# A state-space layer on one core: products with B three steps ahead of their decay instead of two

## The chip, the cores and the metric

The kernel runs on one core of a Trainium2 chip. The metric is the device time of one execution in microseconds (us). Everything is in fp32.

## The reference

The input is `x`, eight images of 128 channels by 128 by 128 pixels. Two layers follow each other. The first (a dilated convolution, a two-dimensional Fourier transform, attention between channels and a gate in the frequency domain) is left as it is by the change. The second layer is what matters:

```python
y = conv2d(x, conv_w, 3x3, padding 1) + conv_b
seq = y.reshape(B * H * W, 8, 16)            # every pixel-row stretch of 128 values: 8 tokens of 16
xi, z = split(seq @ in_proj_w.T)             # 32 and 32 channels
xc = silu(causal_conv1d(xi, 4 taps))
dt, Bm, Cm = split(xc @ x_proj_w.T, [1, 16, 16])
dt = softplus(dt * dt_proj_w + dt_proj_b)
h = 0
for t in range(8):                           # 32 channels x 16 states
    h = exp(dt[t] * A) * h + dt[t] * Bm[t] * xc[t]
    ys[t] = sum(h * Cm[t], over the states)
out = ((ys + D * xc) * silu(z)) @ out_proj_w.T
return x + silu(group_norm(out))
```

The recurrence over eight tokens is done for every pixel position. Per token there are three elementwise products or sums over 32 channels x 16 states: the decay `exp(dt*A) * h`, the sum with the injected `dt*x*B`, and the weighting with C.

## The kernel before, in words

The second layer (`layer1`) walks over 256 blocks of four image rows. A block is `N = 512` columns, and its 512 rows of state (32 channels x 16 states) are held as four groups of 128 partitions. Two groups make one tile of 128 x 1024, so the eight tokens are cut into sixteen steps `s` of two groups each: token `s // 2`, and the first or second pair of groups by `k = s % 2` (`GP = 2`).

For each step these are the operations, and the names that the text uses:

- `spreads(das, upss)` (its product is line 800). TensorE spreads `dt` over channels and states with the matrix `m_a`, into the PSUM tile `da`; and `u = dt * x` with the matrix `m_u`, into the PSUM tile `ups`. The moving operand of both is `du`, where each of the four groups has 32 partitions of its own, with eight rows of `dt` and eight of `u` in the first sixteen. A product uses the sixteen rows from `a = (k * GP + q) * 32`, for `q` 0 and 1. So a spread of one decay and one injection is four products of 16 rows with 512 columns.
- `exps` (line 805): ScalarE takes the exponential of `da` in place.
- `inject` (line 815): VectorE multiplies `ups` with B (`bb`, laid out by DMA) into a new SBUF tile `h`.
- `decay` (lines 829 and 831): VectorE multiplies `da` with the `h` of the step two before.
- `add` (line 839 on VectorE, or 837 on GpSimd for the steps 4, 7 and 10): adds the decayed state to the injected `h`.
- `weigh` (line 845): GpSimd multiplies `h` with C (`cc`) into `hc`; `last_decay` (line 850) is its counterpart for the last token, on VectorE; `collect` (line 866) sums `hc` over the states on TensorE.

The steps 14 and 15 have no injection of their own, since the last token's injected part is summed another way (`end_products`, `ends_sum`, `ends_inputs`). There are fourteen decays (2 to 15) and fourteen injections (0 to 13) in a block.

The order on every engine is written out by hand. `step(i, s)` for s from 2 to 11 issues the spread with the decay of step s+1 and an injection further ahead, the other TensorE work that is laid into this step (projections of the next block, gathers, convolution taps of the block three ahead), then VectorE's decay, sum and injection for the step. `seam(i)` writes out the end of block i (decays 12 to 15) together with the first injections of block i+1.

Buffers set the waits. `ups` has one PSUM buffer, so a spread's injection products wait until the injection before them was read by VectorE. `da` has two buffers, shared with the x and z projections (lines 736 and 745). `h` has six SBUF buffers; `pm`, for convolution, projections and transposes, has one PSUM buffer. The DMA transfers that lay out `du`, `bb` and `cc` are issued from one queue in the order of the code: `lay_du` and `lay_states` for the next block in steps 6 and 10 and at the seam.

Of the kernel before, what the change touches and what calls it, by code (L numbers as in the profile page):

```python
# [589 lines left out]
def layer1(ctx, tc, x1, w1, c1, out):  # L590
# [22 lines left out]
    def cf(name):  # L613
        at, n = C1[name]
        return ct[:, at:at + n]
# [21 lines left out]
    taps = cf("taps").rearrange("p (k l) -> p k l", l=L)  # L637
# [41 lines left out]
    wk1 = ctx.enter_context(tc.tile_pool(name="l1_w1", bufs=1))  # L679
    wk2 = ctx.enter_context(tc.tile_pool(name="l1_w2", bufs=2))  # L680
    wk3 = ctx.enter_context(tc.tile_pool(name="l1_w3", bufs=3))
    hp = ctx.enter_context(tc.tile_pool(name="l1_h", bufs=6))
    hcp = ctx.enter_context(tc.tile_pool(name="l1_hc", bufs=7))
    p_u = ctx.enter_context(tc.tile_pool(name="l1_pu", bufs=1, space=PSUM))
    p_a = ctx.enter_context(tc.tile_pool(name="l1_pa", bufs=2, space=PSUM))
# [10 lines left out]
    def live(i):  # L696
        return 0 <= i < nb
# [4 lines left out]
    def load(i):  # L702
        b, r = blocks[i]
        if r % CH == 0:
            lo, hi = max(0, r - 1), min(H, r + CH + 1)
            xin = wk2.tile([P, CH + 2, W], F32, name="xin")
            nc.sync.dma_start(xin[:, :hi - lo, :], x1[b][:, lo:hi, :])
            xins[b, r // CH] = xin, lo
        st8[i]["xin"] = xins[b, r // CH]
# [20 lines left out]
    def pair():  # L730
        return p_a.tile([P, GP, N], F32, name="da")
# [55 lines left out]
    def spreads(das, upss):  # L787

        todo = []
        for m, name, k0, steps in ((m_a, "da", 0, das), (m_u, "ups", 0, upss)):  # L790
            for i, s in steps:
                if not live(i):
                    continue
                d, t, k = st8[i], s // GP, s % GP
                d[name, s] = pair() if name == "da" else p_u.tile([P, GP, N], F32, name="ups")
                for q in range(GP):
                    a = (k * GP + q) * 32
                    todo.append((d[name, s][:, q], m[a:a + 16, :], d["du", t // LP][a:a + 16, t % LP, :]))
        for o, w, v in todo:
            nc.tensor.matmul(o, w, v, start=True, stop=True)  # L800

    def exps(i, s):
        if live(i):
            da = st8[i]["da", s]
            nc.scalar.activation(da, da, AF.Exp)  # L805

    def state_row(i, name, t):
        return st8[i][name, t // LP][:, t % LP:t % LP + 1, :].broadcast_to([P, GP, N])

    def inject(i, s):  # L810
        if not live(i):
            return
        d = st8[i]
        h = hp.tile([P, GP, N], F32, name="h")
        nc.vector.tensor_mul(h, d["ups", s], state_row(i, "bb", s // GP))  # L815
        d["h", s] = h
# [24 lines left out]
    def weigh(i, s, t):  # L841

        d = st8[i]
        hc = hcp.tile([P, GP, N], F32, name="hc")
        nc.gpsimd.tensor_mul(hc, d["h", s], state_row(i, "cc", t))  # L845
        d["hc", t * GP + s % GP] = hc

    def last_decay(i, s):
        d = st8[i]
        nc.vector.tensor_mul(d["hc", s], d["da", s], d["hc", s])  # L850
# [7 lines left out]
    def ends_inputs(i, hf):  # L858
        d = st8[i]
        nc.vector.tensor_mul(d["yps"], d["yps"], d["u", hf])  # L860
# [40 lines left out]
    def norm_of(b):  # L901

        mv = wk2.tile([P, 2], F32, name="mv")
        gmv = wk2.tile([P, 2], F32, name="gmv")
        dv = wk2.tile([P, 1], F32, name="dv")
        sc = wk2.tile([P, 1], F32, name="sc")
        bi = wk2.tile([P, 1], F32, name="bi")
        nc.vector.bn_aggr(mv, stats[b])
        ps = misc().rearrange("p a b -> p (a b)")
        nc.tensor.matmul(ps[:, 0:2], cf("group"), mv, start=True, stop=True)  # L910
        nc.vector.tensor_copy(gmv, ps[:, 0:2])
        nc.vector.tensor_sub(dv, mv[:, 0:1], gmv[:, 0:1])
        nc.vector.tensor_mul(dv, dv, dv)
        ps = misc().rearrange("p a b -> p (a b)")
        nc.tensor.matmul(ps[:, 0:1], cf("group"), dv, start=True, stop=True)
        nc.vector.tensor_scalar(sc, ps[:, 0:1], gmv[:, 1:2], GN_EPS, ALU.add, ALU.add)
        nc.scalar.activation(sc, sc, AF.Sqrt)
        nc.vector.reciprocal(sc, sc)
        nc.vector.tensor_mul(sc, sc, wf("gn_w"))
        nc.vector.tensor_mul(bi, gmv[:, 0:1], sc)  # L920
        nc.vector.tensor_sub(bi, wf("gn_b"), bi)
        tails.extend((b, r, sc, bi) for r in range(0, H, RB))
# [22 lines left out]
    def step(i, s):  # L945

        now, nxt = live(i), live(i + 1)
        if s == 2:
            if live(i + 4):
                load(i + 4)  # L950
            if live(i - 2) and blocks[i - 2][1] + RB == H:
                norm_of(blocks[i - 2][0])
        spreads([(i, s + 1)], [(i, s + 2)])
        exps(i, s + 1)

        if s == 2:
            if nxt:
                project_dt(i + 1, 0)
            if live(i - 1):
                collect(i - 1, 7)  # L960
        elif s == 3:
            if live(i - 1):
                collect(i - 1, 6)
                skip(i - 1, 1)
            if nxt:
                project_bc(i + 1, 0)
        elif s == 4 and nxt:
            project_dt(i + 1, 1)
        elif s == 5:
            if now:  # L970
                ends_sum(i, 0)
            if nxt:
                project_bc(i + 1, 1)
        elif s == 6:
            if now:
                skip(i, 0)
            if live(i - 1):
                project_out(i - 1, 0, 4)
        elif s == 7 and now:
            collect(i, 1)  # L980
        elif s == 8 and live(i - 1):
            project_out(i - 1, 4, 8)
        elif s == 9 and now:
            collect(i, 2)
        elif s == 11 and now:
            collect(i, 3)
        if s in CONV and live(i + 3):
            conv(i + 3, *CONV[s])

        if now:  # L990
            decay(i, s)
            if s != 4:
                add(i, s)
            inject(i, s + 2)
            if s == 5:
                ends_inputs(i, 0)
            if s == 11:
                gated(i, 0)
        if s == 3 and live(i - 1):
            gated(i - 1, 1)  # L1000

        if now:
            if s == 2:
                end_products(i, 0)
            else:
                weigh(i, s - 1, (s - 1) // GP)
            if s == 4:
                add(i, s)
            if s == 7:
                end_products(i, 1)  # L1010
        if s in (3, 4) and nxt:
            inputs(i + 1, s - 3)
        if s == 9 and "active" in fin:
            last_sum()

        if s == 3 and now:
            lay_states(i, 1, 1)
        elif s == 6 and nxt:
            lay_du(i + 1, 0)
            lay_states(i + 1, 0, 0)  # L1020
        elif s == 8 and tails:
            last_load()
        elif s == 10 and nxt:
            lay_states(i + 1, 0, 1)

    def seam(i):


        now, nxt = live(i), live(i + 1)

        def taps(k0, k1):
            if live(i + 3):
                conv(i + 3, k0, k1)

        spreads([(i, 13)], [(i + 1, 0)])
        exps(i, 13)
        if now:
            ends_sum(i, 1)
            decay(i, 12)
            add(i, 12)  # L1040
            weigh(i, 11, 5)
            weigh(i, 12, 7)
        if nxt:
            lay_states(i + 1, 1, 0)
        taps(5, 6)
        if "loaded" in fin:
            last_act()
        if live(i + 2):
            project_x(i + 2)
        if now:  # L1050
            decay(i, 13)
            add(i, 13)
            weigh(i, 13, 7)
        inject(i + 1, 0)
        if live(i + 2):
            project_z(i + 2)
        spreads([(i, 14)], [(i + 1, 1)])
        exps(i, 14)
        if now:
            ends_inputs(i, 1)  # L1060
        inject(i + 1, 1)
        taps(6, 8)
        spreads([(i, 15)], [(i + 1, 2)])
        exps(i, 15)
        if live(i - 1):
            keep(i - 1)
        inject(i + 1, 2)
        if now:
            collect(i, 4)
            last_decay(i, 14)  # L1070
        taps(8, 9)
        if now:
            weigh(i, 12, 6)
            last_decay(i, 15)
        spreads([(i + 1, 2)], [(i + 1, 3)])
        exps(i + 1, 2)
        inject(i + 1, 3)
        if now:
            collect(i, 5)
            weigh(i, 13, 6)  # L1080
        if live(i + 3):
            turn(i + 3)
        if nxt:
            lay_du(i + 1, 1)
# [95 lines left out]
```

## Time and profile before

| what | value |
|---|---|
| time | 14902.07 us, median of 3 runs (14893.55 to 14902.99) |
| TensorE products busy | 96% of the span |
| GpSimd busy | 87% |
| VectorE busy | 85% |
| ScalarE busy | 56% |
| first and last product with `m_u` | 2068.9 us and 14740.4 us |

Shares are of the whole span, and the first layer, some 2000 us, has other limits than the second. The shares inside the second layer are read from windows of its own. A product in the trace is an instruction with a start and a modelled end; one fp32 product of the program appears as two such instructions, one after the other.

### The profile page before, as it was taken

The numbers are of one execution on the slowest core, as the hardware profiler recorded it, in microseconds if no ns is written. First come the engines' busy times: TensorE is split into PE (matmuls) and PEld (weight loads), VectorE is DVE, ScalarE is ACT, GpSimd is POOL, SyncE is SP. The second block draws the span as 40 slices with busy tenths as digits, with TensorE's granted clock in tenths as the row PEclk, the third lists the DMA queues.
The fourth block names the chain that finished last, engine by engine and source line by source line (L and its number), as shares of the span: only waits on it lengthen the run. The fifth ranks groups of instructions, "written<-read, shape, count | busy, mean of one in ns | idle before, by whom it ended". The sixth has DMA issues, their size and how long they took to land.

```text
span 14895.3 us, 200912 instructions
## 1 busy us (share of the span) xinstructions
PE 14287.1 (96%) x70696; PEld 5588.1 (38%) x70696; DVE 12683.2 (85%) x12417; ACT 8294.9 (56%) x9234; POOL 12983.2 (87%) x7076
## 2 busy tenths in 40 slices
PE   9999999999999999999999999999999999999996
PEld 6677653333333333333333333333333333333331
DVE  3343359999999999999999999999999999999995
ACT  3354355555555555565655555555555555555553
POOL 6666668989999999999999999999999999999996
PEclk9999999999999999999999999999999999999997
DMA  4444456666666666666666666666666666666665
GB/s 136 139 139 122 129 124 117 120 118 121 130 137 134 137 132 136 133 135 134 135 136 133 136 133 137 133 138 131 137 133 136 132 137 133 134 135 135 136 133 140
DMA packets 1091885, 1976.01 MB, mean 133 GB/s; under 512 B 125760, under 2 KB 256832, under 8 KB 1082688
## 3 DMA queue, kind: packets, MB, share of 16 engines
q1 hardware_dynamic: 1090304, 1960.82, 61.0%
q8 instruction: 563, 9.22, 0.3%
q14 instruction: 442, 3.62, 0.1%
q10 hardware_dynamic: 576, 2.35, 0.0%
HBM read 419.16 MB, written 201.33 MB: 42 GB/s over the span
## 4 chain that ended last, share of the span: by engine, by line
PE 72%; DVE 18%; issue 4%; ACT 4%; DMA 1%; POOL 0%; SPq 0%; DVEq 0%; POOLq 0%; ACTq 0%
PE da L800 19%; PE yps L866 9%; PE ups L800 7%; PE pm L134 7%; DVE da L831 6%; PE m L280 4%; DVE h L839 4%; DVE h L815 4%; PE yps L872 4%; PE pm L752 4%; PE pm L885 3%; PE pm L764 3%; DVE hc L850 2%; PE da L745 2%; PE yps L856 2%
## 5 line engine op out<-in xcount | busy, mean ns | idle before, releaser
L845 POOL TENSOR_TENSOR hc<-h,cc 128x1024 f32<-128x1024 f32 x3584 | 8377.2, 2370 | 427.6 <-DVE h L839 408.5
L805 ACT ACTIVATE da<-da 128x1024 f32<-128x1024 f32 x3584 | 3618.7, 1010 | 4193.3 <-PE ups L800 2491.7
L815 DVE TENSOR_TENSOR h<-ups,bb 128x1024 f32<-128x1024 f32 x3584 | 4368.7, 1219 | 690.1 <-PE ups L800 313.9
L800 PE MATMUL da<-du,m_a 16*128 16x512 f32 x14336 | 4068.1, 644 | 140.5 <-DVE hc L850 135.1
L800 PE MATMUL ups<-du,m_u 16*128 16x512 f32 x14336 | 4114.3, 642 | 2.5 <-DVE h L815 1.4
L839 DVE TENSOR_TENSOR h<-da,h 128x1024 f32<-128x1024 f32 x2304 | 2821.2, 1224 | 79.1
L831 DVE TENSOR_TENSOR da<-da,h 128x1024 f32<-128x1024 f32 x2304 | 2820.1, 1224 | 6.8 <-ACT da L805 3.3
L134 PE MATMUL pm<-xin,l_wt 128*128 128x508 f32 (+1 forms) x4608 | 2412.7, 624 | 177.0 <-ACT xr L890 170.2
L837 POOL TENSOR_TENSOR h<-ah,h 128x1024 f32<-128x1024 f32 x768 | 1818.8, 2368 | 451.2 <-DVE ah L829 409.6
L800 PEld LDWEIGHTS da<-du,m_a 16*128 16x128 f32 x14336 | 1078.4, 184 | 2624.6 <-issue 1002.7
L866 PE MATMUL yps<-hc,l_ct 128*32 128x512 f32 x14336 | 1931.7, 611 | 0.0
L134 PEld LDWEIGHTS pm<-xin,l_wt 128*128 128x128 f32 x4608 | 751.7, 189 | 1620.7 <-issue 1396.0
L800 PEld LDWEIGHTS ups<-du,m_u 16*128 16x128 f32 x14336 | 1124.4, 184 | 380.8 <-DVE h L815 298.2
L805 ACT ACT_TABLE_LOAD x774 | 993.0, 1283 | 30.1 <-PE ups L800 1.3
L829 DVE TENSOR_TENSOR ah<-da,h 128x1024 f32<-128x1024 f32 x768 | 933.1, 1215 | 0.0
L759 POOL TENSOR_TENSOR u<-dt,xc 128x512 f32<-128x512 f32 x512 | 656.0, 1281 | 190.2 <-ACT dt L754 190.2
L866 PEld LDWEIGHTS yps<-hc,l_ct 128*32 128x32 f32 x14336 | 283.6, 108 | 1375.1 <-issue 968.6
L754 ACT ACT_TABLE_LOAD x511 | 655.6, 1283 | 29.6 <-PE pm L752 2.1
L822 POOL TENSOR_TENSOR cb<-bb,cc 128x512 f32<-128x512 f32 x512 | 658.3, 1286 | 11.8 <-DMA cc<-bc 11.8
L885 PEld LDWEIGHTS pm<-m_o,ym 128*128 128x128 f32 x4096 | 517.6, 191 | 317.2 <-issue 316.5
L850 DVE TENSOR_TENSOR hc<-da,hc 128x1024 f32<-128x1024 f32 x512 | 600.6, 1215 | 0.9 <-ACT da L805 0.8
L872 PE MATMUL yps<-xc,m_d 128*128 128x512 f32 x1024 | 584.6, 653 | 0.0
(180 smaller groups left out, 14537.5 us busy)
## 6 DMA issues: line engine op xcount, KB each, us to landing
bb<-bc SPq DMA_DIRECT2D x2048, 256.0 KB
cc<-bc SPq DMA_DIRECT2D x2048, 256.0 KB
du<-dt SPq DMA_DIRECT2D x2048, 64.0 KB
du<-u SPq DMA_DIRECT2D x2048, 64.0 KB
xin<-x SPq DMA_DIRECT2D x152, 768.0 KB
xin<-x SPq DMA_DIRECT2D x112, 640.0 KB
gn<-xr SPq DMA_DIRECT2D x256, 256.0 KB
v<-gn SPq DMA_DIRECT2D x256, 256.0 KB
```

The lines of the kernel that those rows point to most:

```text
L134: nc.tensor.matmul(out[:, a:b, wa:wb], wt[:, t, :], src[:, r + dy + a - base:r + dy + b - base, wa + dx:wb + dx], start=(n == 0), stop=(n ...
L800: nc.tensor.matmul(o, w, v, start=True, stop=True)
L805: nc.scalar.activation(da, da, AF.Exp)
L815: nc.vector.tensor_mul(h, d["ups", s], state_row(i, "bb", s // GP))
L829: nc.vector.tensor_mul(d["ah"], da, before)
L831: nc.vector.tensor_mul(da, da, before)
L837: nc.gpsimd.tensor_add(h, d["ah"], h)
L839: nc.vector.tensor_add(h, d["da", s], h)
L845: nc.gpsimd.tensor_mul(hc, d["h", s], state_row(i, "cc", t))
L866: nc.tensor.matmul(d["yps"][g * DI:(g + 1) * DI], gather[:, t % LP, :], d["hc", GP * t + g // GP][:, g % GP], start=False, stop=(t in (3, ...
L872: nc.tensor.matmul(d["yps"], m_d, d["xc"][:, hf, :], start=False, stop=False, skip_group_check=True)
L885: nc.tensor.matmul(d["pm"][:, j, :], d["ym", hf][:, j * C:(j + 1) * C], m_of[:, hf, :], start=(hf == 0), stop=(hf == NH - 1))
```

## The change

The injection products, and the injection on VectorE, run three steps ahead of the decay that is taken up in the step, instead of two. In step s the spread holds the decay of step s+1 and the injection of step s+3. Step 11, the last of the loop, takes the next block's injection 0 instead of this block's injection 13, and the seam then holds the next block's injections 1 to 4 instead of 0 to 3. In the seam the injections' places move a little: the block statistics (`keep`) come before the second injection of the seam, and the injection 3 before the last decay of step 15. The pool `h` has seven buffers instead of six, for the injected tiles that live a step longer. It is meant to have the injected states ready earlier, with the seam's products prepared before the seam.

```diff
-    hp = ctx.enter_context(tc.tile_pool(name="l1_h", bufs=6))
+    hp = ctx.enter_context(tc.tile_pool(name="l1_h", bufs=7))
@@ step
-        spreads([(i, s + 1)], [(i, s + 2)])
+        ahead = (i, s + 3) if s < 11 else (i + 1, 0)
+        spreads([(i, s + 1)], [ahead])
         exps(i, s + 1)
@@
             decay(i, s)
             if s != 4:
                 add(i, s)
-            inject(i, s + 2)
+        inject(*ahead)
+        if now:
             if s == 5:
                 ends_inputs(i, 0)
@@ seam
-        spreads([(i, 13)], [(i + 1, 0)])
+        spreads([(i, 13)], [(i + 1, 1)])
         exps(i, 13)
@@
-        inject(i + 1, 0)
+        inject(i + 1, 1)
         if live(i + 2):
             project_z(i + 2)
-        spreads([(i, 14)], [(i + 1, 1)])
+        spreads([(i, 14)], [(i + 1, 2)])
         exps(i, 14)
         if now:
             ends_inputs(i, 1)
-        inject(i + 1, 1)
-        taps(6, 8)
-        spreads([(i, 15)], [(i + 1, 2)])
-        exps(i, 15)
         if live(i - 1):
             keep(i - 1)
         inject(i + 1, 2)
+        taps(6, 8)
+        spreads([(i, 15)], [(i + 1, 3)])
+        exps(i, 15)
         if now:
             collect(i, 4)
             last_decay(i, 14)
+            weigh(i, 12, 6)
+        inject(i + 1, 3)
         taps(8, 9)
         if now:
-            weigh(i, 12, 6)
             last_decay(i, 15)
-        spreads([(i + 1, 2)], [(i + 1, 3)])
+        spreads([(i + 1, 2)], [(i + 1, 4)])
         exps(i + 1, 2)
-        inject(i + 1, 3)
+        inject(i + 1, 4)
```

## The prediction

> **What bounds the kernel now.** I read the page first: busy time by engine and the slices. The change lies in the second layer alone, whose first product with B starts at 2068.9 us and whose last is at 14740.4 us. I then took three windows of 1000 us in it; the columns are TensorE, its weight loads, VectorE, ScalarE, GpSimd, clock, DMA share.
>
> ```profile
> PE 14287.1 (96%) x70696; PEld 5588.1 (38%) x70696; DVE 12683.2 (85%) x12417; ACT 8294.9 (56%) x9234; POOL 12983.2 (87%) x7076
> ...
> L800 PE MATMUL da<-du,m_a 16*128 16x512 f32 x14336 | 4068.1, 644 | 140.5 <-DVE hc L850 135.1
> L800 PE MATMUL ups<-du,m_u 16*128 16x512 f32 x14336 | 4114.3, 642 | 2.5 <-DVE h L815 1.4
> ```
>
> ```profile
> 5000.00:6000.00 1000.00, 966.84 (x4653) 330.21 (x4652) 937.92 (x857) 587.32 (x610) 922.68 (x445) 1.00 0.64 134
> 9000.00:10000.00 1000.00, 968.93 (x4674) 331.58 (x4670) 941.87 (x853) 590.59 (x611) 929.93 (x448) 1.00 0.65 136
> ```
>
> TensorE is occupied for 97% at full clock, the other engines for less. To see whether it is occupied by work or by waiting, I took the timeline of TensorE over one block, from the z projection at 9004.59 to the next one at 9053.82: 49.23 us a block. The decisive lines are those of `spreads` (line 800). Columns are start, duration, engine, line, operation, count.
>
> ```profile
> 2068.95 1.13 PE L800 MATMUL ups<-du,m_u 16*128 16x512 f32 x4
> ...
> 9022.38 0.70 PE L800 MATMUL da<-du,m_a 16*128 16x512 f32 x2
> 9022.39 0.70 PE L800 MATMUL ups<-du,m_u 16*128 16x512 f32 x2
> 9022.91 0.59 PE L800 MATMUL da<-du,m_a 16*128 16x512 f32 x2
> 9022.92 0.59 PE L800 MATMUL ups<-du,m_u 16*128 16x512 f32 x2
> 9023.45 1.12 PE L752 MATMUL pm<-xc,m_dt 128*128 128x512 f32 x2
> ...
> 9031.53 1.13 PE L800 MATMUL da<-du,m_a 16*128 16x512 f32 x4
> 9032.66 1.20 PE L800 MATMUL ups<-du,m_u 16*128 16x512 f32 x4
> 9033.79 1.06 PE L866 MATMUL yps<-hc,l_ct 128*32 128x512 f32 x8
> ```
>
> The reader is to see three things. First, each fp32 product is two instructions about 0.53 us apart. Second, at 9022.38 all four products of a spread (two decays, two products with B) run side by side: eight instructions take 1.07 us, no more than the one 128-row product after them and no less than the two lone products at 2068.95, where the next product starts 1.06 us later. Third, at 9031.53 the `ups` pair came late, because its one PSUM buffer was still being read, and the spread took 2.26 us: decays and injections one after the other.
>
> Why do four run at once? The operands of a spread start at row `a = (k * GP + q) * 32` with `k = s % 2`. Before the change the decay of step s+1 goes with the injection of step s+2: an odd step with an even one. One pair sits at rows 0 and 32, the other at 64 and 96. All four groups of 32 rows of the array are in use, one product each.
>
> [...] distinct groups start 0.01 us apart, while the two passes of one product, which share a group, are 0.53 us apart. [...] here the four `da` instructions at 9031.53 all ran before a late `ups`, and at 9022.38 they mixed, so I rely on the trace for order between groups.
>
> **The change part by part.**
>
> (1) Every spread now pairs step s+1 with step s+3, or 12 with the next block's 0, 13 with 1, 14 with 2, 15 with 3, and 2 with 4. Both numbers of each pair have the same parity. The injections now need the same two row groups as the decays in front of them, and the other two groups lie idle. Each group has four passes instead of two: 4 x 0.53 = 2.12, with the edge seen above 2.13 us. No instruction is added; TensorE takes twice as long for the same ones. From the timeline of the block, the fourteen spreads now take, from their first start to that of the next other product: 1.11, 1.08, 1.07, 1.07, 1.33, 1.07, 1.45, 1.69, 2.26, 1.45, 1.07, 1.07, 1.51, 1.07, in all 18.30 us. The excess over 14 x 1.07 = 14.98, which is 3.32 us, is lateness of the `ups` pair. Afterwards: 14 x 2.13 = 29.82. The lateness is not added: an injection starts 1.06 us after the decay anyway, and only the late pair at 9031.53 was 1.13 us behind.
> Cost: 29.82 - 18.30 = +11.52 us a block, on the engine that is occupied for 97%.
>
> (2) What does TensorE still wait for? The rest of the block is 49.23 - 18.30 = 30.93 us, and 1.49 of it are waits with no product running: 0.29 before the z projection (for the sum of step 13), 0.52 before the first decay of the next block (for the last decay of step 14), 0.68 before the first convolution tap (for the copy of the output block out of PSUM). The first two are waits for VectorE, which is occupied 46.42 us of 49.23; with 60 us for a block it has more room, so I take both away: -0.81. The copy depends on the output projection just before the tap, so its 0.68 stays.
>
> (3) The order on VectorE in the seam: the statistics of the previous block (0.68 us) move ahead of the second injection, the injection of step 3 ahead of the last decay of step 15. A normal injection is 1.22 us. Behind the last decay of step 15 stands the PSUM buffer for the decay of step 3, which TensorE wants only after a spread, a gather and the transposes (2.13 + 1.00 + 0.58 = 3.7 us). Hidden by those: zero.
>
> (4) The seventh `h` buffer. An injection three ahead with seven buffers waits for the product with C of the same step, s-4, as two ahead with six does; GpSimd gets no new wait. Zero.
>
> (5) Earlier need of data: the next block's `du` and `bb` for step 0 are read in step 11 instead of the seam. Their eight `du` transfers were issued from 9029.07 to 9034.94 and `bb` from 9035.05 to 9040.09, 4.3 us before the spread of step 11 at 9044.36. The longer spreads of steps 7 to 10 add some 4 us to that margin. The trace's answer gives no time to landing, so I bound the cost between 0 and 1 us a block and take 0, for the margin of 8 us. Second halves are read in step 5 rather than 6: they are issued from 9009.83 on and read after 9024; zero.
>
> Sum: +11.52 - 0.81 = +10.71 us a block, 59.94 in place of 49.23. With 256 blocks: 2742 us. 14902 + 2742 = 17644 us.
>
> **The rivals.**
>
> *The step loop becomes the bound as well (0.10).* If every late `ups` stays late by as much (3.32), and no wait is absorbed, a block takes 29.82 + 30.93 + 3.32 = 64.07 us; +14.84 x 256 = 3799, so 18700 us. For it: the one `ups` buffer still ties each spread to the injection before. Against: VectorE's step is 3.53 us start to start (9014.74 to 9018.27), and TensorE's becomes 4.3.
>
> *The row groups don't matter and the order pays (0.04).* Should products of one group overlap after all, what is left is the seam. VectorE sits idle 0.80 and 1.15 us there for `ups`, which now would come a spread earlier; TensorE loses its 0.52 wait and some of the 3.32 us. With half of the lateness gone: 0.52 + 1.66 = 2.18 us x 256 = 558, so 14344 us; faster. Against: two passes of one product never overlap in the trace.
>
> *Nothing changes (0.01).* The kinds of instructions stand in nearly the same order on each engine, so with free overlap and a seam bound elsewhere it would be 14902 us. Against: the 0.52 wait.
>
> **How the numbers follow.** The main case has 0.85. Within it, if the 0.68 goes too, a block takes 59.26 and the time is 17470; if all 1.49 stay, 60.75 and 17851; with the 1 us of (5) on top about 18110. The wait before the tap and the block that I read may be off by some tenths, which is 26 us for each 0.1. Range 17300 to 18060: it leaves out the fast rivals (0.05), the heavy one (0.10) and the edges. Faster 0.04, same 0.01, slower 0.95.
>
> **What would show it.** Right: in the timeline each spread has four `da` instructions, then four `ups` 1.06 us later, 2.13 us in all; a block near 60 us; TensorE still at 97% or more; VectorE and GpSimd down to about 46.4 / 60 = 77% and 45.7 / 60 = 76% of it; no wait before the next block's first decay. Wrong: `da` and `ups` starting 0.01 us apart as before; or spreads over 3 us long with TensorE waiting on line 815; or the clock below 1.00 in the windows.

## The result, and the profile after

| | before | after |
|---|---|---|
| time, median | 14897.81 us (14892.87 to 14902.99) | 17282.84 us (17253.24 to 17298.81) |
| ratio | 1 | 1.1599, 95% interval 1.1578 to 1.1619 |
| block, from one z projection to the next, median of 255 | 49.23 us | 57.02 us |
| the same, mean without the first and last five | 49.42 us | 58.72 us |
| at half TensorE clock, blocks 4 to 253 | 58 us | 887 us |

The last row adds up the trace's records of the granted clock; in both traces each record is 1.0 or 0.5. The block times are taken from the starts of the z projection (line 745).

The page of the changed kernel, with TensorE's busy time, the chain of work that ended last (before, TensorE had 72% of that chain and VectorE 18%), and the groups of `spreads` and `inject`:

```profile
PE 16850.8 (97%) x70696; PEld 6521.1 (38%) x70696; DVE 12786.7 (74%) x12417; ACT 8324.7 (48%) x9234; POOL 12991.7 (75%) x7076
...
PE 95%; ACT 3%; DMA 1%; DVE 1%; issue 0%; POOL 0%; SPq 0%; POOLq 0%; DVEq 0%; ACTq 0%
...
L815 DVE TENSOR_TENSOR h<-ups,bb 128x1024 f32<-128x1024 f32 x3584 | 4376.7, 1221 | 2637.9 <-PE ups L800 2129.3
...
L800 PE MATMUL da<-du,m_a 16*128 16x512 f32 x14336 | 4148.6, 656 | 40.2 <-DVE h L839 3.1
L800 PE MATMUL ups<-du,m_u 16*128 16x512 f32 x14336 | 3769.3, 602 | 4.9 <-DVE h L815 4.9
```

The same instructions are there in the same number. TensorE is now nearly the whole chain, and VectorE sits idle in front of its injections (2637.9 us) because the products for them are late. The windows in the second layer (TensorE, weight loads, VectorE, ScalarE, GpSimd, clock, DMA share):

```profile
5000.00:6000.00 1000.00, 984.64 (x3905) 340.74 (x3904) 796.60 (x722) 497.24 (x513) 775.64 (x374) 0.97 0.57 113
9000.00:10000.00 1000.00, 984.64 (x3966) 343.19 (x3964) 810.22 (x735) 505.84 (x522) 787.63 (x379) 0.98 0.57 114
```

TensorE is occupied for 98%, but at a mean clock of 0.97 and 0.98 instead of 1.00. A spread in the timeline:

```profile
9001.99 1.13 PE L800 MATMUL da<-du,m_a 16*128 16x512 f32 x4
9002.95 1.02 PE L800 MATMUL ups<-du,m_u 16*128 16x512 f32 x4
9003.90 1.12 PE L752 MATMUL pm<-xc,m_dt 128*128 128x512 f32 x2
```

Decays first and injections after them: 1.91 us from the first start to the next product's. Cut into narrower windows, the same spread shows its passes, two row groups in each:

```profile
9001.99 0.70 PE L800 MATMUL da<-du,m_a 16*128 16x512 f32 x2
9002.52 0.59 PE L800 MATMUL da<-du,m_a 16*128 16x512 f32 x2
9002.95 0.59 PE L800 MATMUL ups<-du,m_u 16*128 16x512 f32 x2
9003.38 0.59 PE L800 MATMUL ups<-du,m_u 16*128 16x512 f32 x2
```

The starts are 0.53, 0.43, 0.43 and (to the next product) 0.52 us apart. A pass costs 0.43 us; about 0.1 us more is paid at the start and at the end of the whole group, once each. A spread before the change had two passes in each row group with both edges: 1.07 us. (The spread of six passes further down fits the same price.)

The reduced clock, at one place of many. First the timeline of step 7 and 8 of a block, then the window that begins after the convolution tap:

```profile
5163.87 1.13 PE L800 MATMUL da<-du,m_a 16*128 16x512 f32 x4
5164.83 1.02 PE L800 MATMUL ups<-du,m_u 16*128 16x512 f32 x4
5165.79 1.16 PE L885 MATMUL pm<-m_o,ym 128*128 128x128 f32 x8
5167.62 2.07 PE L134 MATMUL pm<-xin,l_wt 128*128 128x512 f32 x2 [0.68 <-ACT xr L890]
5169.62 2.08 PE L800 MATMUL da<-du,m_a 16*128 16x512 f32 x4
5171.49 1.92 PE L800 MATMUL ups<-du,m_u 16*128 16x512 f32 x4
```

```profile
5169.62:5178.30 8.68, 8.68 (x23) 2.58 (x24) 2.88 (x3) 1.01 (x1) 6.95 (x5) 0.54 0.79 176
```

The tap and the spread after it take twice as long (2.07 in place of 1.12; 3.72 in place of 1.91), at a granted clock of 0.54. The records put about 90 of the 100 such stretches in blocks 4 to 253 between 38 and 42 us after the z projection before them, which is this place.

### The profile page after: what moved, and what is told of

Its sections match the earlier page's. It is cut to its first block, busy times and chain, and to the rows that moved or that the text cites. A ratio compares the mean times of both kernels' runs of the same rounds, so it can differ in the third digit from the quotient of the medians.

```text
span 17284.5 us, 200914 instructions
## 1 busy us (share of the span) xinstructions
PE 16850.8 (97%) x70696; PEld 6521.1 (38%) x70696; DVE 12786.7 (74%) x12417; ACT 8324.7 (48%) x9234; POOL 12991.7 (75%) x7076
## 4 chain that ended last, share of the span: by engine, by line
PE 95%; ACT 3%; DMA 1%; DVE 1%; issue 0%; POOL 0%; SPq 0%; POOLq 0%; DVEq 0%; ACTq 0%
PE da L800 23%; PE ups L800 18%; PE pm L134 14%; PE yps L866 11%; PE m L280 4%; PE yps L872 3%; PE pm L752 3%; PE yps L856 3%; PE pm L885 3%; PE da L736 3%; PE pm L764 3%; ACT xc L738 2%; PE ps L386 1%; ACT xr L890 1%; PE pm L726 1%; PE pf L488 1%
## 5 line engine op out<-in xcount | busy, mean ns | idle before, releaser
L815 DVE TENSOR_TENSOR h<-ups,bb 128x1024 f32<-128x1024 f32 x3584 | 4376.7, 1221 | 2637.9 <-PE ups L800 2129.3
L800 PE MATMUL da<-du,m_a 16*128 16x512 f32 x14336 | 4148.6, 656 | 40.2 <-DVE h L839 3.1
L800 PE MATMUL ups<-du,m_u 16*128 16x512 f32 x14336 | 3769.3, 602 | 4.9 <-DVE h L815 4.9
L134 PE MATMUL pm<-xin,l_wt 128*128 128x508 f32 (+1 forms) x4608 | 2569.9, 660 | 176.6 <-ACT xr L890 170.2
L800 PEld LDWEIGHTS ups<-du,m_u 16*128 16x128 f32 x14336 | 1403.8, 189 | 1771.2 <-issue 1321.6
L866 PE MATMUL yps<-hc,l_ct 128*32 128x512 f32 x14336 | 2029.2, 640 | 0.0
L134 PEld LDWEIGHTS pm<-xin,l_wt 128*128 128x128 f32 x4608 | 792.2, 199 | 1738.5 <-issue 1513.2
L752 PE MATMUL pm<-xc,m_dt 128*128 128x512 f32 x1024 | 580.6, 649 | 1.5 <-issue 0.8
```

Of the source, the lines that this page charges most:

```text
L134: nc.tensor.matmul(out[:, a:b, wa:wb], wt[:, t, :], src[:, r + dy + a - base:r + dy + b - base, wa + dx:wb + dx], start=(n == 0), stop=(n ...
L752: nc.tensor.matmul(ps, m_dtf, d["xc"][:, hf, :], start=True, stop=True)
L866: nc.tensor.matmul(d["yps"][g * DI:(g + 1) * DI], gather[:, t % LP, :], d["hc", GP * t + g // GP][:, g % GP], start=False, stop=(t in (3, ...
```

## The experiments

### Three steps ahead, row groups apart

`u` is laid out two groups further round than `dt`, and the injection products start from there; everything else is the changed kernel.

```diff
-            for k, v in ((0, d["dt", hf]), (8, d["u", hf])):
-                nc.sync.dma_start(du[q * DI + k:q * DI + k + 8], v[q * DI:(q + 1) * DI, :])
+            for k, v, to in ((0, d["dt", hf], q), (8, d["u", hf], (q + GP) % NG)):
+                nc.sync.dma_start(du[to * DI + k:to * DI + k + 8], v[q * DI:(q + 1) * DI, :])
...
-        for m, name, k0, steps in ((m_a, "da", 0, das), (m_u, "ups", 0, upss)):
+        for m, name, k0, steps in ((m_a, "da", 0, das), (m_u, "ups", GP, upss)):
...
-                    a = (k * GP + q) * 32
+                    a = (k * GP + q + k0) % NG * 32
```

> The changed kernel with one thing moved: u is laid out two groups further round than dt (group q at rows ((q+2)%4)*32), so the injection products of a spread use the two row groups that its decay products leave free. Same instructions in the same order. Theory (row groups are the whole loss): spreads back from 1.91 to about 1.07 us, no half-clock stretches beyond a few, a block between 46.5 (VectorE's busy time) and 49.2 us, time 14300 to 14950. Rival (the order three ahead itself costs: longer chains, late data): spreads of 1.07 but a block well above 50 us, time nearer 17000 than 15000.

Measured: 14726.73 us, ratio to the kernel before 0.9887 (0.9871 to 0.9904). Block 48.57 us; 48 us at half clock. The spreads in the timeline:

```profile
9001.61 0.70 PE L800 MATMUL da<-du,m_a 16*128 16x512 f32 x2
9001.62 0.70 PE L800 MATMUL ups<-du,m_u 16*128 16x512 f32 x2
9002.14 0.59 PE L800 MATMUL da<-du,m_a 16*128 16x512 f32 x2
9002.15 0.59 PE L800 MATMUL ups<-du,m_u 16*128 16x512 f32 x2
9002.68 1.98 PE L134 MATMUL pm<-xin,l_wt 128*128 128x508 f32 x4
```

1.07 us again, all four groups at once. The whole loss of the change, clock included, is in which rows the operands lie; the order three steps ahead costs nothing.

### Two steps ahead, same row groups

The same edit on the kernel before.

> The kernel before, with u laid out two groups further round, so that two steps ahead now gives decay and injection the same row groups. Theory: spreads of 1.91 us, a block of 57 to 58 us, half-clock stretches as in the changed kernel, time 17100 to 17500. Rival (the row groups matter only together with the new order): time within 300 us of 14900.

Measured: 17263.1 us, ratio 1.1593 (1.1576 to 1.161). Block 57.56 us, 553 us at half clock. The counterpart: the old order with shared row groups is as slow as the change. Its block is 0.54 us longer than the change's, and its timeline still has the wait before the next block's first decay, of 0.47 us at 9055.52.

### The first tap in step 9

```diff
-    CONV = {8: (0, 1), 9: (1, 2), 10: (2, 3), 11: (3, 5)}
+    CONV = {9: (0, 2), 10: (2, 3), 11: (3, 5)}
```

> The changed kernel with the first convolution tap moved from step 8 to step 9, so that it does not wait in step 8 for the output block to leave PSUM. Theory [...]: the wait goes, the stretches nearly all go (887 us at half clock in the second layer become under 200), block 56.3 us, time 16550 to 16850. Rival (half-filled spreads alone lower the clock): only the wait goes, 256 x 0.68 = 174 us, stretches stay, time about 17110.

Measured on the changed kernel: 16674.49 us, ratio 1.1194 (1.1177 to 1.1211). Block 56.14 us, 68 us at half clock.

```profile
5000.00:6000.00 1000.00, 995.98 (x4088) 349.33 (x4084) 832.25 (x756) 522.66 (x539) 810.09 (x391) 1.00 0.59 118
```

The stretches do go. What made them is not settled by this: with the tap the idle time went and the mixture of products changed.

### Each injection product twice

```diff
-        for o, w, v in todo:
+        for o, w, v in todo + todo[GP:] * (len(todo) > GP):
             nc.tensor.matmul(o, w, v, start=True, stop=True)
```

> The changed kernel with each injection product of a spread with decays issued twice into the same place (the second writes the same values). Price by itself: if a pass in the same row group costs 0.43 us and the edges of a spread 0.2 us once, a spread takes 0.2 + 6 x 0.43 = 2.78 us, a block about 69.0 us at full clock, time about 20300 plus more half-clock stretches. If each pass costs 0.53 us as the prediction took it, a spread takes about 3.0 us and a block about 72. If passes of one group overlap, 1.91 and 57.

Measured in one execution: 25438.04 us. At full clock a spread of six passes:

```profile
9013.03 1.13 PE L800 MATMUL da<-du,m_a 16*128 16x512 f32 x4
9014.00 1.88 PE L800 MATMUL ups<-du,m_u 16*128 16x512 f32 x8
9015.81 1.13 PE L752 MATMUL pm<-xc,m_dt 128*128 128x512 f32 x2
```

2.78 us, as 0.2 + 6 x 0.43 says. But the total is some 5000 us over what this gives, because the clock falls:

```profile
5000.00:6000.00 1000.00, 989.57 (x3187) 345.65 (x3186) 526.55 (x475) 325.55 (x336) 506.00 (x243) 0.75 0.38 74
```

TensorE is occupied for 99% here, and its clock is the lowest of the study: 11496 us at half clock. The kernel with the late tap is occupied for 99.6% at a clock of 1.00. So in these kernels neither idle time nor the occupied share decides when the clock halves.

### The order in the seam alone

The kernel before, two steps ahead, with the change's order in the seam: the block statistics ahead of the second injection, the last decay of step 14 ahead of the third, the third ahead of the last decay of step 15.

```diff
+        if live(i - 1):
+            keep(i - 1)
         inject(i + 1, 1)
         taps(6, 8)
         spreads([(i, 15)], [(i + 1, 2)])
         exps(i, 15)
-        if live(i - 1):
-            keep(i - 1)
-        inject(i + 1, 2)
         if now:
             collect(i, 4)
             last_decay(i, 14)
+            weigh(i, 12, 6)
+        inject(i + 1, 2)
         taps(8, 9)
         if now:
-            weigh(i, 12, 6)
             last_decay(i, 15)
```

> The kernel before, two steps ahead, with the change's order in the seam alone: the block statistics ahead of the seam's second injection, the last decay of step 14 ahead of the third, the injection of the third ahead of the last decay of step 15. Theory (what e1 wins over the kernel before is the order in the seam, not the third step of lead): the 0.52 us wait before the next block's first decay goes, block 48.5 to 48.8, time 14700 to 14790. Rival (it is the lead): wait and time as before, 14850 to 14900.

Measured: 14743.64 us, ratio 0.9899 (0.9885 to 0.9912); block 48.65 us. The first experiment's ratio was 0.9887 (0.9871 to 0.9904). The two intervals overlap: nearly all that the change could win is the order in the seam. The third step of lead has 0.08 us a block left to it, which is not clear of the noise. It doesn't make the injections less late either: the fourteen spreads of a block take 18.25 us in the first experiment (median of blocks 60 to 199), and 18.27 both here and in the kernel before.

### The late tap with the row groups apart

Three kernels: the first experiment with the tap in step 9, the kernel before with it, and the seam order with it.

> Three steps ahead with u two groups round (as e1) and the first tap in step 9 (as e3). Theory: TensorE's wait of 0.68 us before the tap goes, but VectorE is idle for only 1.7 us of a block of 48.57, so at most that is to be won: block 47.6 to 48.6, time 14480 to 14730. If VectorE's chain bounds the block already, no change from e1 (14727).

> The kernel before with the first tap in step 9 alone. Its spreads use all four row groups and its clock is full, so no half-clock stretch is to be cured: at most 0.68 us of 49.23 a block, time 14720 to 14900. Were the tap's wait bad for the clock there too, the gain would exceed 256 x 0.68 = 174 us.

> As e7, with the first tap in step 9. If seam and tap are what there is to win and the lead of three steps is worth nothing, the time is within 0.3% of that of e5; if the lead is needed once TensorE has no wait, e5 is faster by more.

Measured: 15070.37 us, ratio 1.0119 (1.0105 to 1.0133); 15336.62 us, 1.0298 (1.0284 to 1.0312); 15122.22 us, 1.0154 (1.014 to 1.0168). None of them gains: what cured the clock in the changed kernel spoiled it here, with 543, 727 and 587 us at half clock. The comparison that the third was meant for (0.3% to the first) came out at 0.34% and tells nothing, since both lose clock. The second one's timeline before a stretch of half clock:

```profile
9002.07 1.13 PE L800 MATMUL da<-du,m_a 16*128 16x512 f32 x4
9003.20 1.20 PE L800 MATMUL ups<-du,m_u 16*128 16x512 f32 x4
9004.32 1.07 PE L866 MATMUL yps<-hc,l_ct 128*32 128x512 f32 x8
...
9006.77 1.16 PE L885 MATMUL pm<-m_o,ym 128*128 128x128 f32 x8
9008.11 1.13 PE L800 MATMUL da<-du,m_a 16*128 16x512 f32 x4 [0.18 <-DVE h L839]
9009.24 1.33 PE L800 MATMUL ups<-du,m_u 16*128 16x512 f32 x4
9010.50 1.94 PE L866 MATMUL yps<-hc,l_ct 128*32 128x512 f32 x8
```

In these steps the injections are late, so that decays and injections run one after the other here too, and the tap, a product of 128 full rows, no longer stands between them. That is read from this trace alone; wider products in the first of the three kernels test it below.

This gave a second theory: that the clock falls where few rows of the array are in use. Up to here no run shows it: it is my guess from the products of 16 rows in these timelines, and the next experiment tests it.

### Thirty-two rows instead of sixteen

The products take rows 16 to 31 of each group as well, which hold zeros. The sums are the same, and the products take the same time: the two pairs of a decay 0.70 and 0.59 us with 16 rows (first experiment, at 9001.61) and with 32 (the fastest kernel below, at 9022.79).

```diff
-                    todo.append((d[name, s][:, q], m[a:a + 16, :], d["du", t // LP][a:a + 16, t % LP, :]))
+                    todo.append((d[name, s][:, q], m[a:a + 32, :], d["du", t // LP][a:a + 32, t % LP, :]))
...
+    dus = [wk1.tile([P, LP, N], F32, name=f"du{hf}") for hf in range(NH)]
+    for du in dus:
+        nc.vector.memset(du, 0.0)
...
-        d = st8[i]
-        du = wk2.tile([P, LP, N], F32, name="du")
+        d, du = st8[i], dus[hf]
```

> The changed kernel with the spreads' products taken over 32 rows instead of 16; rows 16 to 31 of each group hold zeros (du in two lasting buffers, zeroed once). Same instructions, same results, more cells of the array in use. Theory [...]: the half-clock stretches go, 887 us at half clock become under 150, block 57.0 us throughout, time 16800 to 16950. Rival (idle time or few products, not the cells in use, lower the clock): as before, 17250 to 17320.

Measured on the changed kernel: 16843.86 us, ratio 1.1314 (1.1298 to 1.1329); 44 us at half clock, block 57.02 us as in the changed kernel.

```profile
5000.00:6000.00 1000.00, 983.96 (x4026) 344.39 (x4024) 821.39 (x744) 511.34 (x528) 799.86 (x386) 1.00 0.54 116
```

The idle time, the waits and the order are those of the changed kernel, TensorE's share is the same 98%, and the clock is 1.00 in place of 0.97. This is an intervention: here the rows in use, zeros or not, decide (887 us at half clock with 16 rows, 44 with 32). It also separates the loss: 17283 - 16844 = 439 us of it is clock, the rest the longer spreads.

> As e5 (three ahead, u two groups round, first tap in step 9) with 32 rows. Theory: e5's 543 us at half clock go; what is left of the tap's wait is then won if VectorE lets it: block 47.9 to 48.6, time 14560 to 14740. Rival: the stretches stay, 15070.

> As e1 (three ahead, u two groups round, tap in step 8) with 32 rows. The clock is full there already, so nothing changes but the few stretches at image ends: 14690 to 14740. Were wider products slower in themselves, it would show here.

With row groups apart: 14795.71 us with the late tap, 0.9939 (0.9926 to 0.9953); 14689.81 us without it, 0.9867 (0.9853 to 0.988), the fastest kernel of the study. The stretches went in both (10 us left), so the wider products cure the clock with the late tap as well. Still, the late tap is slower, which I had not expected: its block is 48.99 us against 48.57. TensorE's 0.68 us wait is gone in its timeline, but VectorE's injection of step 10 waits longer, 0.66 us with the late tap (first fence) against 0.23 without it (second):

```profile
9040.05 1.23 DVE L818 TENSOR_TENSOR h<-ups,bb 128x1024 f32<-128x1024 f32 x1 [0.66 <-PE ups L803]
```

```profile
9027.21 1.23 DVE L818 TENSOR_TENSOR h<-ups,bb 128x1024 f32<-128x1024 f32 x1 [0.23 <-PE ups L803]
```

The 0.43 us between them match the difference of the blocks, 0.42. In the timelines the products of this injection, taken in step 10, stand behind two taps in step 9 instead of one; that this is the cause is read and not tested. What is shown is that TensorE's wait of 0.68 us can go without a gain. In the windows of the fastest kernel VectorE is occupied for 95.5% and TensorE for 98%, and the shares do not say which of them sets the block.

## Why the prediction was right or wrong

The direction, the cause and the order of size were right; the time lies 17 us below the range and 361 us below the forecast. Two terms were off, in opposite directions, and that the time came so near the range is luck: at full clock, as with 32 rows, the same order takes 16844 us, 456 us below it.

**Step (1), the price of a pass, failed in size.** The working took the distance of 0.53 us between the two passes of a spread as the price of each further pass, hence 2.13 us. That distance holds an edge. A further pass cost 0.43 us, and the spread took 1.91. 14 x (2.13 - 1.91) = 3.1 us a block too much, 788 us in all. The lines that could have told were in the timeline before, at the taps:

```profile
9041.19 1.12 PE L134 MATMUL pm<-xin,l_wt 128*128 128x508 f32 x2
9042.24 0.70 PE L800 MATMUL da<-du,m_a 16*128 16x512 f32 x2
...
9046.86 1.97 PE L134 MATMUL pm<-xin,l_wt 128*128 128x508 f32 x4
9048.76 0.70 PE L800 MATMUL da<-du,m_a 16*128 16x512 f32 x2
```

One tap, two instructions, took 1.05 us to the next product's start, and two taps, four instructions, took 1.90: two more cost 0.85 and not 1.06.

**A term was missing: the clock.** The prediction named a clock below 1.00 only as a sign of error and gave it no price; that sign came. In blocks 4 to 253, 887 us ran at half clock against 58 before, and half of the difference, 415 us, estimates what that cost. The run with 32 rows gives 439 for it.

**Together they account for the result.** 57.02 - 49.23 = 7.79 us x 256 = 1994; with 415 for the clock 2409, against 2385 measured. From the forecast: 2742 - 788 + 415 = 2369.

**Step (2) had the right amount, and for one of its waits the wrong reason.** The 0.52 us wait before the next block's first decay is gone, as is the 0.29 before the z projection, and the 0.68 before the tap stayed. The prediction took the first two away because VectorE would have more room. For the z projection that fits: the wait is gone wherever the block is long, in the second experiment too, and stays at 0.30 us with the seam's order alone. For the 0.52 it doesn't: with as long a block and the old order, in the second experiment, 0.47 us of it stay, and with the seam's order alone it goes at a block of 48.65 us. The order in the seam removes it, and step (3) had priced that at zero; that the sum was right here is luck. A small new wait came: the decay after the z projection now starts 1.27 us after it (9037.66 to 38.93) instead of 1.06, because TensorE waits there for ScalarE's x. It is the 0.2 us by which the block is longer than the corrected sum.

**Steps (4) and (5) held.** Waits of the injection for `bb` are 29.0 us in all against 25.9, and for GpSimd 9.9 against 38.0, by the waits of line 815.

**The rivals.** That every late injection stays late: refuted, each spread in the timeline from 9001 to 9058 us is 1.91 to 1.92 us. That row groups don't matter: refuted from both sides by the first two experiments. (The prediction's argument against it, that two passes of one product never overlap in the trace, isn't in its lines: a first pass of 0.70 us, its end being modelled, is followed by the next after 0.53.) With the row groups apart the order does pay, but 0.66 us a block and not the 2.18 of the fast rival: the 0.52 us wait goes, and the lateness of the injections, of which the rival counted half as won, stays whole.

## What to carry to other kernels

Where small products run side by side in one array, the rows they come from are part of the schedule: shifting the order by one step can pair products that share a row group (here a spread took 1.91 us in place of 1.07), and no count of instructions, waits or buffers shows it. Price a further pass by what a longer run of the same kind adds (0.43 us here), and not by a gap that holds the group's edges (0.53). And look at the clock beside the busy share: here a TensorE occupied for 98% ran at a clock of 0.97 with products of 16 rows, and operands padded to 32 with zero rows brought it to 1.00, with the products no longer in themselves (0.70 and 0.59 us either way).

## What the runs showed of the hardware

In the traces before and after, every record of the granted clock is full or half. What I had not expected is that the clock did not follow the time in which TensorE is occupied. With the products twice that was 99% at a clock of 0.75, with the late tap 99.6% at 1.00; with 32 rows in place of 16, in the same order and with the same 98%, the clock went from 0.97 to 1.00. How few rows are too few was not shown, and no kernel varied the columns.
